# A decoder layer's self-attention: values of two head pairs in one product of 256 columns

## The chip, the core and the metric

The kernel runs on one core of a Trainium2 chip. The metric is device time in microseconds (us) of one execution, smaller is better. A core has five engines that run side by side, each through its own list of instructions in order: TensorE (PE; its weight loads are shown apart as PEld), VectorE (DVE), ScalarE (ACT), GpSimd (POOL) and SyncE (SP), which only starts transfers. They meet by semaphores. Transfers between the core's memories and HBM share 16 DMA engines. PE's results land in PSUM, which PE writes and VectorE and ScalarE read.

## What is computed

One decoder layer in float32: self-attention, cross-attention and a feed-forward block, each followed by a layernorm of input plus result. x has 2 batches of 1024 tokens and 256 channels; there are 16 heads of 64. Only the self-attention is touched:

```python
q = split_heads(x @ Wq)      # Wq, Wk, Wv: 256 x 1024
k = split_heads(x @ Wk)
v = split_heads(x @ Wv)
q = apply_rope(q); k = apply_rope(k)
sim = einsum('bid,bjd->bij', q, k) * scale
attn = softmax(where(causal, sim, -inf), axis=-1)
out = einsum('bij,bjd->bid', attn, v) ... @ Wo + bo
```

## The kernel before

Self-attention goes by *pairs* of heads: 16 pairs, 8 for each batch (`keys`). A pair's columns of Wq, Wk and Wv are 128 wide. The work of a pair is cut into named steps, and the order of all steps on all engines is written out by hand: `steps` is one *period*, a list of (step, further), and period n runs each step for pair n + further. A period holds the scores of pair n, the attention products of pair n - 1 and the projections of pairs n + 1 and n + 2. A text `opening` gives the order before the first full period, and `ending` the order of the last two pairs; steps done there are skipped in the periods. The steps that matter here, with the pair's number in front when one is meant (2e0 is step e0 of pair 2):

- `L`: loads the pair's weights (SP, one DMA for each of Wk, Wq, Wv). `Pk`, `Pq` with a half 0 or 1: projections of 512 tokens on PE (L270). `Ek`, `Eq`: ScalarE copies them out of PSUM to `raw` (L278). `d`, `c`, `s`, `a`: the rope, by a DMA that swaps rows into `turned` and by GpSimd (L296 to L305).
- `Pv0`, `Pv4`: values of tokens 0 to 511 and 512 to 1023 (`values`, L313): 4 tiles of 128 tokens, two products each, with 128 columns of Wv moving. `Ev0`, `Ev4`: ScalarE copies them to the tile `v` (L322), one buffer. `w` (`spread`): stores `v` to HBM (`v_d`, 512 KB). `l` (`copies`, L332): four DMAs of 512 KB bring it back in another layout, `v4`, two issued by ScalarE's queue and two by SP.
- `S0` to `S4`: scores (L353), both heads side by side on two halves of PE's rows. `T`: VectorE masks them and takes the row's extreme (L367), out of two pairs of PSUM banks. `X`: ScalarE's exponentials (L375). `R`: VectorE transposes into `pT` (L384).
- `V0` to `V7`: attention products (L424), 244 small ones a pair from `v4` and `pT` into four PSUM banks, 64 in V0 and V1, 64 in V2 and V3, 116 in V4 to V7; scores of the next pair stand between these three bursts (each product of the program leaves two matmul and two weight-load records). `O`, `M`, `W`: the result is copied, scaled and stored to `attn_d`. `A` loads it for the closing of batch 0, whose `po_proj` products (L496) run in periods 10 and later.

PSUM has a ring of four banks (tag "t") that projections, values, attention products and po_proj take in turn; a product waits until the bank four turns back was copied out. `begin` (L210) starts a DMA on SP; `gate` holds some of them until the attention products V1 or V7 of a pair (or some scores) are through.

`split` cuts a product's columns into 2, or for projections 4, and takes each cut from the pair's budget `pieces`, refilled at V7:

```python
n = 4 if most == 4 and left[0] >= 8 else 2
if left[0] < n - 1 or last - first < n * P:
    return [slice(first, last)]
left[0] -= n - 1
```

`turn_x` turns x into `x_ts` on PE (L193), four blocks of 512 tokens in three buffers.

Of the kernel before, what the change touches and what calls it, by code (L numbers as in the profile page):

```python
# [8 lines left out]
F32 = mybir.dt.float32  # L9
# [7 lines left out]
P, R32 = 128, 32  # L17
B, T, C = 2, 1024, 256
H, D = 16, 64
# [3 lines left out]
NT = T // P  # L23
NC = C // P
NP = INNER // P
NF = FF // P
NB = 512
# [7 lines left out]
def decoder_layer(  # L35
# [24 lines left out]
    V, A, G, TE = nc.vector, nc.scalar, nc.gpsimd, nc.tensor  # L60
# [5 lines left out]
    dram = ctx.enter_context(tc.tile_pool(name="dram", bufs=2, space=DRAM))  # L66
# [58 lines left out]
    keys = [(b, hp) for b in range(B) for hp in range(NP)]  # L125
# [3 lines left out]
    e1 = early.enter_context(tc.tile_pool(name="early1", bufs=1, side="right"))  # L129
    e2 = early.enter_context(tc.tile_pool(name="early2", bufs=2, side="right"))  # L130
    with (
# [76 lines left out]
        def begin(dst, src):  # L208

            ins = nc.sync.dma_start(dst, src)  # L210
            if gate:
                tc.add_manual_dep(ins.ins, gate.pop().ins.name, after, reason="the outputs' instructions come first")
# [3 lines left out]

        pieces = [2, 1, 15, 13, 11, 10, 11, 12, 13, 12, 8, 9, 8, 8, 9, 0]
        left = [pieces[0]]  # L220

        def split(first, last, most):

            n = 4 if most == 4 and left[0] >= 8 else 2
            if left[0] < n - 1 or last - first < n * P:
                return [slice(first, last)]
            left[0] -= n - 1
            step = -(-(last - first) // n // P) * P
            return [slice(m, min(m + step, last)) for m in range(first, last, step)]
# [18 lines left out]
        class Pair:  # L248
            def __init__(self, n):
                self.n, (self.b, self.hp) = n, keys[n]  # L250
                self.pp, self.raw, self.turned, self.p, self.spans, self.marks = {}, {}, {}, {}, {}, {}
                self.w = self.kq = self.v = self.out = None


            def weights(self):
                if self.w is not None:
                    return
                self.w = e2.tile([P, NC, 3, P], F32, tag="w", name="w_pair")
                cols = slice(self.hp * P, (self.hp + 1) * P)
                for i, w in enumerate((L0_attn_Wk, L0_attn_Wq, L0_attn_Wv)):  # L260
                    begin(self.w[:, :, i, :], w.rearrange("(c p) n -> p c n", p=P)[:, :, cols])


# [41 lines left out]
                    E.tensor_tensor(dst, dst, tiles_of(self.turned[n][:, i, :], odd), ALU.add)  # L305


            def values(self, n):
                pv = self.pp["v", n] = ring.tile([P, NT // 2, P], F32, tag="t", name="pp_v")
                for i in range(NT // 2):  # L310
                    toks = slice(i * P, (i + 1) * P)
                    for c in range(NC):
                        TE.matmul(  # L313
                            pv[:, i, :], x_ts[self.b, 2 * n // NT][:, c, toks], self.w[:, c, 2, :],
                            start=(c == 0), stop=(c == NC - 1),
                        )

            def kept(self, n):
                if self.v is None:
                    self.v = e1.tile([P, NT, P], F32, tag="v", name="v")  # L320
                    self.v_d = dram.tile([4, R32, NT * P], F32, tag="v", name="v_d")
                A.copy(self.v[:, n : n + NT // 2, :], self.pp["v", n])  # L322

            def spread(self):

                begin(self.v_d.rearrange("r k e -> (r k) e"), self.v.rearrange("p n d -> p (n d)"))

            def copies(self):

                self.v4 = s1.tile([P, K4, P], F32, tag="v4", name="v4")  # L330
                for r in range(4):
                    (nc.scalar, nc.sync)[r % 2].dma_start(  # L332
                        self.v4[r * R32 : (r + 1) * R32, :, :].rearrange("k (c n) d -> k c (n d)", c=4),
                        self.v_d.rearrange("c k e -> k c e"),
                    )


# [116 lines left out]
            def store(self):  # L454
                begin(
                    attn_d[self.b][self.hp], self.out.rearrange("p t q -> p (t q)")
                )

        class Closing:


# [46 lines left out]


        steps = [  # L510
            ("Eq0", 1), ("Ek0", 1), ("Ev4", 1), ("Eq1", 1), ("a0", 0), ("R40", -1), ("S0", 0), ("T00", 0), ("T01", 0),
            ("s1", 0), ("V0", -1), ("a1", 0), ("V1", -1), ("S1", 0), ("GS1", 0), ("d0", 1), ("V2", -1), ("T10", 0),
            ("V3", -1), ("T11", 0), ("S2", 0), ("GS2", 0), ("B", -2), ("X00", 0), ("V4", -1), ("V5", -1), ("R00", 0),
            ("X01", 0), ("R01", 0), ("c0", 1), ("Z", -15), ("X11", 0), ("T20", 0), ("V6", -1), ("T21", 0), ("V7", -1),
            ("w", 1), ("X10", 0), ("X20", 0), ("O1", -1), ("S3", 0), ("R10", 0), ("O0", -1), ("R11", 0), ("Q", -1),
            ("s0", 1), ("O3", -1), ("T31", 0), ("l", 0), ("C", 0), ("O2", -1), ("X31", 0), ("Pk1", 1), ("T30", 0),
            ("I", -1), ("Pv0", 2), ("X30", 0), ("M", -2), ("R20", 0), ("Ek1", 1), ("d1", 1), ("R31", 0), ("Ev0", 2),
            ("D", -1), ("S4", 0), ("R30", 0), ("Pq1", 2), ("L", 3), ("W", -2), ("A", 0), ("c1", 1), ("X21", 0),
            ("Pq0", 2), ("T41", 0), ("Pk0", 2), ("X41", 0), ("T40", 0), ("R21", 0), ("R41", 0), ("X40", 0), ("Pv4", 2),
        ]  # L520

        pairs = [Pair(n) for n in range(len(keys))]
        acts = {
            "P": lambda a, x: a.values(int(x[1])) if x[0] == "v" else a.project(x[0], int(x[1])),
            "E": lambda a, x: a.kept(int(x[1])) if x[0] == "v" else a.evacuated(x[0], int(x[1])),
            "d": lambda a, x: a.swap(int(x)),
            "c": lambda a, x: a.cosine(int(x)),
            "s": lambda a, x: a.sine(int(x)),
            "a": lambda a, x: a.rotated(int(x)),
            "w": lambda a, x: a.spread(),  # L530
            "l": lambda a, x: a.copies(),
            "L": lambda a, x: a.weights(),
            "S": lambda a, x: a.scores(int(x)),
# [13 lines left out]


        opening = """
            1L 0Pk0 0Ek0 0Pq0 0Eq0 0H 0h 0Pq1 0c0 0d0 0s0 0a0 0Pk1 0Pv4 0Pv0 0Eq1 0S0 0Ek1 0Ev0 1Pk1 0T00 0d1 0Ev4 0T01  # L550
            1Pq1 0X00 0c1 0s1 0X01 1Eq1 1Ek1 1Pv0 0a1 0S1 2L 0R00 0w 0R01 1d1 1Pv4 1c1 1Pq0 1Pk0 0T10 0T11 0S2 1Ev4 0T21
            1Eq0 1Ek0 1d0 0X10 1Ev0 0l 1s1 1w 0X11 2Pq1 0T20 0R10 0S3 0R11 0X21 0X20 0T30 2Pk0 1a1 0T31 0X30 1c0 0S4
            0X31 0R20 1s0 0R30 0R21 1a0 2Eq1 0T40 3L 2Pv4 0T41 2Pv0 0X40 0X41 2Ek0 0R31 0R40 2Pq0 2Ev4 1S0 0R41 1T00
            2Eq0 2Ev0 0V0 1T01 0V1 2d0 0V2 1S1 1T11 0V3 1X00 0V4 0V5 1T10 1S2 1X01 1X11 1R00 0V6 0V7 2w 1X10 0O0 1T20
            1T21 1S3 1R10 1R01 0O1 2c0 1l 1X20 1T31 2Pk1 0O3 1T30 0O2 3Pv4 0Q 2Ek1 1S4 2c1 1X30 2s0 1X21 3Pq1 1R20 3Ev4
            3Pv0 2a0 1R11 3Pk0 0I 1T41 2d1 1R30 1X31 3Pq0 1T40 2S0 1R21 1X41 1X40 1R31 1R40 0D 1R41 2T00 3Ek0 2s1 3Eq1
            4L 2a1 3Eq0 3Ev0 1V0 1V1 3d0 0B 2T01 2X00 1V2 2S1 1V3 1V4 2T10 2T11 1V5 2R00 2S2 2X01 2T20 2T21 1V6 2X11
            2R01 1V7 3c0
        """


        ending = """
            14X10 14X20 14S3 13O0 15s0 15a0 12M 14X21 14R11 14R20 14l 13O1 14T31 14T30 14R21 14X30 14X31 15Pk1 15w 13Q 13I
            14S4 15Ek1 14T40 12W 4C 14T41 14X41 13O2 14R10 15a0 15d1 14R31 13O3 14R30 13D 14X40 15c1 14R40 14R41 15S0 4Y
            15T00 14V0 15T01 15X00 14V1 14V2 15X01 15s1 15a1 14V3 5A 13B 15R00 15S1 15T10 14V4 6A 15X10 14V5 15T11 15S2
            14V6 14V7 15X11 15R01 15T21 15l 15T20 13M 14O3 15S3 7A 15X20 5C 15X21 15R10 15T30 14O0 15T31 15R11 15X30
# [12 lines left out]
        def do(n, step):  # L579
            if (n, step) in done or not 0 <= n < (NT if step in closing else len(keys)):  # L580
                return
            if step in closing:
                b, act = closing[step]
                act(closings[b][n])
            elif step == "H":
                turn_x(0, NH, NT)
            elif step == "h":
                for keep in kept_later:
                    keep()
            elif step == "N":  # L590
                load_cross(n)
            elif step == "n":
                turn_context()
            else:
                if n == last and step[0] == "O":
                    pairs[n].gathered_scaled(int(step[1]))
                elif n == 0 and step in ("c0", "s0", "a0"):
                    {"c": pairs[0].cosine, "s": pairs[0].sine, "a": pairs[0].rotated}[step[0]](0, V)
                else:
                    acts[step[0]](pairs[n], step[1:])  # L600

                if (n, step) in ((NP - 3, "S4"), (NP, "Pv0")):
                    turn_x(1, *((0, NH) if step == "S4" else (NH, NT)))
                if step == "V7" and n + 1 < len(keys):
                    left[0] = pieces[n + 1]
                if step == "W":
                    for f in later.get(n, ()):
                        f()
            done.add((n, step))
# [683 lines left out]
```

## Time and profile before

| what | us |
|---|---|
| median of 3 runs (788.04 to 791.29) | 790.05 |
| the profiled execution | 789.92 |
| its span | 788.2 |
| first attention product (V0 of pair 0) | 51.0 |
| V0 of pairs 1, 2, 3 | 81.1, 111.4, 141.5 |
| V0 of pairs 11, 12, 13, 14, 15 | 384.6, 417.1, 450.1, 475.6, 507.5 |
| PE, records of scores, attention products, kq projections, values (chain share) | 18%, 17%, 14%, 7% |
| a store of `v` (512 KB), issue to landing, median | 8.4 |
| a load to `v4` (512 KB), issue to landing, median | 11.8 (ScalarE's queue), 11.0 (SP's) |

A page of the profile gives each engine's busy time and share; the chain of waits follows the end back from instruction to whatever released it, so that its shares are of time that nothing else hid. A timeline lists the instructions in order (start, length, engine, line, output<-inputs, shapes, count), with the idle time before one in brackets and who ended it; "issue" is a wait for nothing that the profile shows. Ends of matmuls are modelled, so PE's pace is read from starts. The granted clock of PE was 0.996 over the span.

### The profile page before, as it was taken

The page shows a single profiled execution, that of the slowest core. Times are in us where ns is not written, and L with a number is a line of the kernel's source. Part 1 is how long each engine was busy: PE and PEld are TensorE (multiplying, and loading weights), DVE is VectorE, ACT ScalarE, POOL GpSimd, SP SyncE. Part 2 cuts the span into 40 slices and gives each one's busy share as a digit, 9 for nine tenths or more (in the row PEclk, how much of TensorE's full clock was granted, in tenths as well). Part 3 has the DMA queues.
Part 4 walks back from the last instruction along what each step waited for, and adds up shares of the span by engine and source line. Part 5 has one row for each costly group of instructions (what it writes and reads, how often), then busy time and mean ns, then how long its engine had stood idle before and what let it go on. Part 6 is the DMA issues. An engine that isn't in the chain of part 4 may idle for free.

```text
span 788.2 us, 27062 instructions
## 1 busy us (share of the span) xinstructions
PE 762.3 (97%) x11328; PEld 615.8 (78%) x11328; DVE 552.5 (70%) x1299; ACT 390.0 (49%) x1249; POOL 391.0 (50%) x407
## 2 busy tenths in 40 slices
PE   8999999999999999999999998999999999999996
PEld 6565788888888888888887877688967888787755
DVE  2578679669669669677786687815576678758673
ACT  2555566566566566554555553400565665552130
POOL 3733665665575575573754854034024333371665
PEclk9999999999999999999999999999999999999999
DMA  5356377477377577576483656775069988861131
GB/s 200 121 163 173 123 206 196 156 197 201 133 190 198 173 227 190 174 202 178 141 241 112 180 153 175 178 249 178 1 197 238 213 214 204 194 159 54 54 107 53
DMA packets 141413, 131.97 MB, mean 167 GB/s; under 512 B 79554, under 2 KB 117996, under 8 KB 141292
## 3 DMA queue, kind: packets, MB, share of 16 engines
q1 hardware_dynamic: 133132, 100.09, 46.2%
q10 hardware_dynamic: 6624, 25.96, 11.0%
q0 software_dynamic: 1536, 4.20, 1.5%
q8 instruction: 89, 1.46, 0.8%
q14 instruction: 32, 0.26, 0.1%
HBM read 81.68 MB, written 31.76 MB: 144 GB/s over the span
## 4 chain that ended last, share of the span: by engine, by line
PE 81%; POOL 5%; DVE 5%; DMA 4%; issue 3%; ACT 1%; ACTq 0%; POOLq 0%; SPq 0%; DVEq 0%
PE ps_scores L353 18%; PE po_self L424 17%; PE pp_kq L270 14%; PE pp_v L313 7%; PE po_proj L496 6%; PE po_cross L1079 5%; PE ps_cross L1009 5%; PE pp_h L942 2%; POOL comp L877 2%; PE po_ffn L957 2%; POOL e_all L1037 2%; DMA turned<-raw 1%; DVE reach L847 1%; DMA over<-inv_d 1%; PE ps_vo L768 1%
## 5 line engine op out<-in xcount | busy, mean ns | idle before, releaser
L375 ACT ACTIVATE p<-p,neg 128x768 f32<-128x768 f32 (+7 forms) x256 | 196.3, 768 | 148.7 <-DVE neg L367 147.0
L367 DVE CUSTOM_DVE_ANT_0 p<-ps_scores,fence 128x512 f32<-128x512 f32 (+7 forms) x256 | 179.5, 751 | 104.6 <-PE ps_scores L353 104.3
L384 DVE STREAM_TRANSPOSE pT<-p 128x512 f32<-128x512 f32 (+7 forms) x256 | 175.8, 740 | 6.0 <-PE po_self L424 4.1
L424 PE MATMUL po_self<-pT,v 32*64 32x128 f32 (+7 forms) x7808 | 151.1, 290 | 10.2 <-issue 7.7
L424 PEld LDWEIGHTS po_self<-pT,v 32*64 32x64 f32 x7808 | 135.2, 131 | 31.6 <-issue 23.1
L353 PE MATMUL ps_scores<-kq 64*128 64x256 f32 (+3 forms) x1060 | 150.8, 410 | 0.3 <-POOL kq L305 0.3
L353 PEld LDWEIGHTS ps_scores<-kq 64*128 64x128 f32 x1060 | 99.5, 186 | 35.5 <-issue 18.4
L270 PE MATMUL pp_kq<-xT,w_pair 128*128 128x256 f32 (+2 forms) x532 | 118.9, 376 | 1.0 <-ACT xT L194 0.8
L296 POOL TENSOR_TENSOR kq<-raw,cos 128x256 f32<-128x256 f32 (+1 forms) x93 | 82.2, 912 | 60.2 <-ACT raw L278 60.2
L301 POOL TENSOR_TENSOR turned<-turned,sin 128x1024 f32<-128x1024 f32 x31 | 73.2, 2363 | 78.3 <-DMA turned<-raw 78.2
L270 PEld LDWEIGHTS pp_kq<-xT,w_pair 128*128 128x128 f32 x532 | 88.8, 191 | 23.7 <-issue 10.7
L1028 ACT ACTIVATE e_all<-ps_cross,top 128x77 f32<-128x77 f32 x256 | 79.0, 339 | 53.0 <-DVE top L1020 51.0
L1037 POOL TENSOR_TENSOR e_all<-e_all,inv 128x616 f32<-128x616 f32 x32 | 38.8, 1216 | 91.0 <-DVE inv L1035 91.0
L305 POOL TENSOR_TENSOR kq<-kq,turned 128x256 f32<-128x256 f32 (+1 forms) x93 | 82.4, 914 | 1.5
L107 POOL TENSOR_TENSOR rs<-ve,neg_half 128x1 f32<-128x1 f32 x48 | 26.8, 560 | 109.8 <-DVE ve L105 109.5
L1079 PE MATMUL po_cross<-packed,pT 128*128 128x256 f32 (+1 forms) x320 | 72.1, 380 | 0.3 <-issue 0.3
L1009 PE MATMUL ps_cross<-wqk,x1T 128*128 128x308 f32 x256 | 69.9, 425 | 0.3 <-ACT e_all L1028 0.3
L1079 PEld LDWEIGHTS po_cross<-packed,pT 128*128 128x128 f32 (+1 forms) x320 | 60.0, 190 | 9.3 <-issue 0.7
L313 PEld LDWEIGHTS pp_v<-w_pair,xT 128*128 128x128 f32 x512 | 61.1, 192 | 4.0 <-issue 2.5
L313 PE MATMUL pp_v<-w_pair,xT 128*128 128x128 f32 x512 | 62.2, 276 | 0.0
L1009 PEld LDWEIGHTS ps_cross<-wqk,x1T 128*128 128x128 f32 x256 | 47.2, 190 | 17.5 <-ACT e_all L1028 1.3
L1028 ACT ACTIVATION_READ_ACCUMULATOR e_all<-ps_cross,top 128x1 f32 x256 | 56.4, 220 | 0.0
(129 smaller groups left out, 789.2 us busy)
## 6 DMA issues: line engine op xcount, KB each, us to landing
turned<-raw SPq DMA_DIRECT2D x64, 256.0 KB, 5.1
v<-v_d ACTq DMA_DIRECT2D x32, 512.0 KB, 11.8
v<-v_d SPq DMA_DIRECT2D x32, 512.0 KB, 11.0
part_d<-part ACTq DMA_DIRECT2D x14, 640.0 KB, 4.0
pT<-part_d SPq DMA_DIRECT2D x56, 160.0 KB, 3.9
v_d<-v SPq DMA_DIRECT2D x16, 512.0 KB, 8.4
over<-inv_d SPq DMA_DIRECT2D x32, 256.0 KB, 4.4
attn_d<-out_pair SPq DMA_DIRECT2D x14, 512.0 KB, 4.1
```

The costliest lines, as they stand in the source:

```text
L270: TE.matmul(pp[:, cols], self.w[:, c, "kq".index(of), :], x_ts[self.b, n][:, c, cols], start=(c == 0), stop=(c == NC - 1),)
L296: E.tensor_tensor(dst, tiles_of(self.raw[n][:, i, :], odd), tiles_of(cos[:, n * NB : (n + 1) * NB], odd), ALU.mult)
L305: E.tensor_tensor(dst, dst, tiles_of(self.turned[n][:, i, :], odd), ALU.add)
L313: TE.matmul(pv[:, i, :], x_ts[self.b, 2 * n // NT][:, c, toks], self.w[:, c, 2, :], start=(c == 0), stop=(c == NC - 1),)
L353: ins = TE.matmul(self.ps[j][:, cols], self.kq[rows, 1, t * P : (t + 1) * P], self.kq[rows, 0, cols.start - at : cols.stop - at], start=Tr ...
L367: V.tensor_tensor_reduce(p[:, span], self.ps[j][:, span], fences[t % 2][:, T - (t + 1) * P :], -SCALE, -MASKED, ALU.add, ALU.min, neg[:, i ...
L375: A.activation(p[:, span], p[:, span], AF.Exp, bias=neg[:, i : i + 1], scale=-1.0, accum_out=self.sums[:, j, t : t + 1],)
L384: V.transpose(p_t[:, first : first + t * step + 1 : step, :], self.p[g, j][:, span].rearrange("p (n k) -> p n k", k=P),)
L424: ins = TE.matmul(self.po[r][j * D : (j + 1) * D, t:, :], self.v4[rows, NT * k + a, j * D : (j + 1) * D], p_t[rows, first : first + (NT - ...
L1009: TE.matmul(ps[:, g, : Q * S], self.x_t[:, c, :], wqk[:, c, self.b, h : h + Q, :].rearrange("p h s -> p (h s)"), start=(c == 0), stop=(c = ...
L1028: A.activation(self.e[:, hh * HH + h, :], sc[:, g, q, :], AF.Exp, bias=top[:, g, q : q + 1], accum_out=sums[:, h : h + 1],)
L1079: TE.matmul(po, self.p_t[:w, k, :], of[:w, k, :], start=(k == 0), stop=(k == NK - 1))
```

## The change

Two neighbouring pairs make a `Couple`. Its Wv columns, 256 wide, are loaded at once (`i`, one buffer) and are the moving side of one product, so that a product gives 128 tokens' values of both pairs. A period makes half of the tokens for a couple: for an even pair tokens 0 to 511, for an odd one 512 to 1023, in two steps of two token tiles each (`p0`, `p2`), copied out by `e0`, `e2` into `v`, which holds both pairs' half, and stored by `w` into a `v_d` for both pairs. A couple's first pair needs both halves, so the value steps run one pair further ahead (3 instead of 2 for the products, 2 instead of 1 for the store). The halves for pair 9 are done together at `p2` and `e2`, since the block of x that they read is turned later in that period. The budgets of cuts are larger, a four-way cut needs 3 left and not 8, the blocks of batch 1 are turned at S4 of pairs 4 and 6, and the opening is written anew for the couples.

```diff
--- before.py
+++ after.py
@@ pieces and their cuts
-        pieces = [2, 1, 15, 13, 11, 10, 11, 12, 13, 12, 8, 9, 8, 8, 9, 0]
+        pieces = [2, 13, 18, 17, 14, 16, 15, 16, 17, 17, 12, 13, 12, 16, 7, 2]
...
-            n = 4 if most == 4 and left[0] >= 8 else 2
+            n = 4 if most == 4 and left[0] >= 3 else 2
@@ class Pair
-                self.w = e2.tile([P, NC, 3, P], F32, tag="w", name="w_pair")
+                self.w = e2.tile([P, NC, 2, P], F32, tag="w", name="w_pair")
...
-                for i, w in enumerate((L0_attn_Wk, L0_attn_Wq, L0_attn_Wv)):
+                for i, w in enumerate((L0_attn_Wk, L0_attn_Wq)):
...
-            def values(self, n):
-                pv = self.pp["v", n] = ring.tile([P, NT // 2, P], F32, tag="t", name="pp_v")
-                for i in range(NT // 2):
-                    toks = slice(i * P, (i + 1) * P)
-                    for c in range(NC):
-                        TE.matmul(
-                            pv[:, i, :], x_ts[self.b, 2 * n // NT][:, c, toks], self.w[:, c, 2, :],
-                            start=(c == 0), stop=(c == NC - 1),
-                        )
-
-            def kept(self, n):
-                if self.v is None:
-                    self.v = e1.tile([P, NT, P], F32, tag="v", name="v")
-                    self.v_d = dram.tile([4, R32, NT * P], F32, tag="v", name="v_d")
-                A.copy(self.v[:, n : n + NT // 2, :], self.pp["v", n])
-
-            def spread(self):
-
-                begin(self.v_d.rearrange("r k e -> (r k) e"), self.v.rearrange("p n d -> p (n d)"))
-
             def copies(self):
...
-                        self.v_d.rearrange("c k e -> k c e"),
+                        couples[self.n // 2].v_d[self.n % 2].rearrange("c k e -> k c e"),
@@ new
+        class Couple:
+            def __init__(self, m):
+                self.b, self.hp = keys[2 * m]
+                self.pp, self.w, self.v_d, self.v = {}, None, None, {}
+
+            def weights(self):
+                if self.w is not None:
+                    return
+                self.w = e1.tile([P, NC, 2 * P], F32, tag="wv", name="w_values")
+                cols = slice(self.hp * P, (self.hp + 2) * P)
+                begin(self.w, L0_attn_Wv.rearrange("(c p) n -> p c n", p=P)[:, :, cols])
+
+            def values(self, n):
+                pv = self.pp[n] = ring.tile([P, 2, 2 * P], F32, tag="t", name="pp_v")
+                for i in range(2):
+                    at = (n + i) * P % NB
+                    for c in range(NC):
+                        TE.matmul(
+                            pv[:, i, :], x_ts[self.b, n // NH][:, c, at : at + P], self.w[:, c, :],
+                            start=(c == 0), stop=(c == NC - 1),
+                        )
+
+            def kept(self, n):
+                h, i = divmod(n, NH)
+                if h not in self.v:
+                    self.v[h] = e1.tile([P, 2, NH, P], F32, tag="v", name="v")
+                A.copy(
+                    self.v[h][:, :, i : i + 2, :].rearrange("p j i d -> p i j d"),
+                    self.pp[n].rearrange("p i (j d) -> p i j d", j=2),
+                )
+
+            def spread(self, h):
+                if self.v_d is None:
+                    self.v_d = dram.tile([2, 4, R32, NT * P], F32, tag="v", name="v_d")
+                begin(
+                    self.v_d.rearrange("j r k e -> (r k) j e")[:, :, h * NB : (h + 1) * NB],
+                    self.v[h].rearrange("p j i d -> p j (i d)"),
+                )
@@ steps of a period (the lines with a changed step)
-            ("Eq0", 1), ("Ek0", 1), ("Ev4", 1), ("Eq1", 1), ("a0", 0), ("R40", -1), ("S0", 0), ("T00", 0), ("T01", 0),
+            ("Eq0", 1), ("Ek0", 1), ("e2", 2), ("Eq1", 1), ("a0", 0), ("R40", -1), ("S0", 0), ("T00", 0), ("T01", 0),
...
-            ("w", 1), ("X10", 0), ("X20", 0), ("O1", -1), ("S3", 0), ("R10", 0), ("O0", -1), ("R11", 0), ("Q", -1),
+            ("w", 2), ("X10", 0), ("X20", 0), ("O1", -1), ("S3", 0), ("R10", 0), ("O0", -1), ("R11", 0), ("Q", -1),
...
-            ("I", -1), ("Pv0", 2), ("X30", 0), ("M", -2), ("R20", 0), ("Ek1", 1), ("d1", 1), ("R31", 0), ("Ev0", 2),
-            ("D", -1), ("S4", 0), ("R30", 0), ("Pq1", 2), ("L", 3), ("W", -2), ("A", 0), ("c1", 1), ("X21", 0),
-            ("Pq0", 2), ("T41", 0), ("Pk0", 2), ("X41", 0), ("T40", 0), ("R21", 0), ("R41", 0), ("X40", 0), ("Pv4", 2),
+            ("I", -1), ("p0", 3), ("X30", 0), ("M", -2), ("R20", 0), ("Ek1", 1), ("d1", 1), ("R31", 0), ("e0", 3),
+            ("D", -1), ("S4", 0), ("R30", 0), ("Pq1", 2), ("i", 4), ("L", 3), ("W", -2), ("A", 0), ("c1", 1), ("X21", 0),
+            ("Pq0", 2), ("T41", 0), ("Pk0", 2), ("X41", 0), ("T40", 0), ("R21", 0), ("R41", 0), ("X40", 0), ("p2", 3),
...
+        couples = [Couple(m) for m in range(len(keys) // 2)]
+        of_couples = {
+            "p0": lambda a, h: a.values(h * NH), "p2": lambda a, h: a.values(h * NH + 2), "e0": lambda a, h: a.kept(h * NH),
+            "e2": lambda a, h: a.kept(h * NH + 2), "w": lambda a, h: a.spread(h), "i": lambda a, h: h or a.weights(),
+        }
@@ opening (its first lines) and ending
-            1L 0Pk0 0Ek0 0Pq0 0Eq0 0H 0h 0Pq1 0c0 0d0 0s0 0a0 0Pk1 0Pv4 0Pv0 0Eq1 0S0 0Ek1 0Ev0 1Pk1 0T00 0d1 0Ev4 0T01
-            1Pq1 0X00 0c1 0s1 0X01 1Eq1 1Ek1 1Pv0 0a1 0S1 2L 0R00 0w 0R01 1d1 1Pv4 1c1 1Pq0 1Pk0 0T10 0T11 0S2 1Ev4 0T21
-            1Eq0 1Ek0 1d0 0X10 1Ev0 0l 1s1 1w 0X11 2Pq1 0T20 0R10 0S3 0R11 0X21 0X20 0T30 2Pk0 1a1 0T31 0X30 1c0 0S4
-            0X31 0R20 1s0 0R30 0R21 1a0 2Eq1 0T40 3L 2Pv4 0T41 2Pv0 0X40 0X41 2Ek0 0R31 0R40 2Pq0 2Ev4 1S0 0R41 1T00
+            1L 0i 0Pk0 0Ek0 0Pq0 0Eq0 0H 0h 0Pq1 0c0 0d0 0s0 0a0 0Pk1 0p0 0p2 0Eq1 0S0 0Ek1 0e0 0e2 1Pk1 0T00 0d1 1p0 0w 1p2 0T01
+            1Pq1 0X00 0c1 0s1 0X01 1Eq1 1Ek1 0a1 0S1 2i 2L 0R00 1e0 1e2 1w 0R01 1d1 2p0 2p2 1c1 1Pq0 1Pk0 0T10 0T11 0S2 2e0 2e2 0T21
+            1Eq0 1Ek0 1d0 0X10 0l 1s1 2w 0X11 2Pq1 0T20 0R10 0S3 0R11 0X21 0X20 0T30 2Pk0 1a1 0T31 0X30 1c0 0S4
+            0X31 0R20 1s0 0R30 0R21 1a0 2Eq1 0T40 3L 3p0 3p2 0T41 0X40 0X41 2Ek0 0R31 0R40 2Pq0 3e0 3e2 4i 1S0 0R41 1T00
...
-            14X10 14X20 14S3 13O0 15s0 15a0 12M 14X21 14R11 14R20 14l 13O1 14T31 14T30 14R21 14X30 14X31 15Pk1 15w 13Q 13I
+            14X10 14X20 14S3 13O0 15s0 15a0 12M 14X21 14R11 14R20 14l 13O1 14T31 14T30 14R21 14X30 14X31 15Pk1 13Q 13I
@@ do()
+            elif (n, step) in ((NP + 1, "p0"), (NP + 1, "e0")):
+                return
+            elif step in of_couples:
+                for one in (step[0] + "0", step) if (n, step) in ((NP + 1, "p2"), (NP + 1, "e2")) else (step,):
+                    of_couples[one](couples[n // 2], n % 2)
...
-                if (n, step) in ((NP - 3, "S4"), (NP, "Pv0")):
-                    turn_x(1, *((0, NH) if step == "S4" else (NH, NT)))
+                if (n, step) in ((NP - 4, "S4"), (NP - 2, "S4")):
+                    turn_x(1, *((0, NH) if n == NP - 4 else (NH, NT)))
```

## The prediction

> **What bounds the kernel now.** I read the page's busy shares first, then the chain of waits in order of time, then the timelines of single engines, then the stretches from one first attention product to the next. PE is busy in 97% of the span and makes up 81% of the chain. Between 1.5 and 465 us the chain is PE nearly without a break, so in self-attention time is PE's own pace, plus what holds PE up.
>
> ```profile
> PE 762.3 (97%) x11328; PEld 615.8 (78%) x11328; DVE 552.5 (70%) x1299; ACT 390.0 (49%) x1249; POOL 391.0 (50%) x407
> PE 81%; POOL 5%; DVE 5%; DMA 4%; issue 3%; ACT 1%; ACTq 0%; POOLq 0%; SPq 0%; DVEq 0%
> ...
> q8 instruction: 89, 1.46, 0.8%
> ```
>
> ```profile
> 37.43 1.80 PE ps_scores L353 x8
> 39.23 1.91 PE pp_kq L270 x4
> 41.14 2.71 PE ps_scores L353 x8
> ...
> 275.29 1.79 PE pp_kq L270 x16
> 277.08 1.79 PE pp_v L313 x16
> 278.87 1.93 PE ps_scores L353 x16
> 280.80 5.38 PE pp_kq L270 x24
> 286.18 1.78 PE pp_v L313 x16
> ...
> 334.12 3.46 PE po_proj L496 x16
> ```
>
> The chain gives paces (start, us, work, records; an f32 product leaves two records). Sixteen value records of 128 columns take 1.79 us, 111.9 ns each. Sixteen records of 256 columns (po_proj) take 3.46, 216.25 each. A projection of 512 columns cut in four (16 records) takes 1.79, and cut in two 8 x 216.25 = 1.73.
>
> What holds PE up within a period is seen in its timeline, at pairs 2 and 7. It is the burst V4 to V7, once split by a hole and once whole:
>
> ```profile
> 123.88 1.34 PE L424 MATMUL po_self<-pT,v 32*64 32x64 f32 x104 [1.02 <-issue]
> ```
>
> ```profile
> 270.06 3.31 PE L424 MATMUL po_self<-pT,v 32*64 32x128 f32 x232
> ```
>
> The hole waits for no other engine. The instruction queue moved 1.46 MB in 89 packets, 16.4 KB each, which at 22,656 PE instructions is 255 instructions a packet: PE waits for its own code. From the start of such a burst to the scores behind it takes 4.28 us at pair 2 (120.87 to 125.15) and 3.24 at pair 7 (270.06 to 273.30). Over pairs 2 to 13 these holes come to about 4 us.
>
> The last view is VectorE at the end of pair 12's period, and the two last full periods as windows (length, then busy us of PE, PEld, DVE, ACT, POOL):
>
> ```profile
> 444.11 3.21 DVE L384 STREAM_TRANSPOSE pT<-p 128x768 f32<-128x768 f32 x3
> 450.18 0.69 DVE L367 CUSTOM_DVE_ANT_0 p<-ps_scores,fence 128x512 f32<-128x512 f32 x1 [2.85 <-PE ps_scores L353]
> ```
>
> ```profile
> 417.10:450.10 33.00, 32.45 (x639) 27.30 (x637) 24.07 (x54) 17.27 (x42) 18.90 (x19) 1.00 0.52 162
> 450.10:475.60 25.50, 24.09 (x588) 19.70 (x586) 22.00 (x50) 14.37 (x37) 14.13 (x14) 1.00 0.56 152
> ```
>
> VectorE ends its transposes at 447.3 and PE starts the next attention products at 450.1. So here PE has the last word by 2.8 us. The period after it has no values left, and there VectorE is busy for 22.0 of 25.5.
>
> **The change, part by part**, against the profiled execution: span 788.2, time 789.92, so 1.7 outside the span. The median of the three runs, 790.05, is 0.1 above it.
>
> *Values.* 512 records of 128 columns become 256 of 256: 512 x 111.9 = 57.3 against 256 x 216.25 = 55.4, all on the chain: -1.9 us.
>
> The Trainium skill (TensorE: Matmul & The Clock Gate, Back-to-back issue gap) puts a warm matmul at its columns over 2.4 GHz plus 2.5 ns, which would make each merge worth 2.5 ns and all 256 of them 0.6 us (an estimate). The rows give 2 x 111.9 - 216.25 = 7.5 ns a merge.
>
> *Cuts.* `pieces` goes from 142 to 207 in sum, and four-way cuts are allowed from 3 left, not 8. Counted in the two programs' order, projections cut in four rise from 9 to 45, those in two fall from 42 to 8; 36 x (1.79 - 1.73) = +2.2. Scores lose 18 products, some 5 ns each: -0.1. Together +2.1, on the chain. What the cuts buy is place: 128 products fewer in values against 65 x 2 more from cuts leave PE's program as long as it was (5742 against 5740 products), and from pair 1 on each pair's attention products start within 0.06 of a 256-instruction block of where they did. So I let the holes stay. Were all lost, -4.1.
>
> The Trainium skill (Runtime: NRT & Kernel Launch, Instruction fetch mechanics) calls a 16 KiB boundary mostly hidden; by that the holes would be nothing and the cuts a plain loss of 2.1. The 1.02 us above is against it.
>
> *One half-couple moves from the end to the opening.* A period now makes half the tokens for two pairs, so both halves must be there before the couple's first pair. Before the first attention product (51.05) stand 96 value records now, 96 x 111.9 = 10.7, and then 64 of the wide ones, 13.8: +3.1 there, and 32 narrow ones (-3.6) fewer in pair 12's period. As sums these are in the first term; what matters is what stands beside them.
> - Opening: PE waits there for VectorE to free score banks: 2.71 us for 8 score records that take 1.92 elsewhere, and 1.80 for 8 that need some 1.6. More PE work ahead covers this: -1.0. Against it, there is one `v` buffer, and ScalarE's copy 2e0 now waits for the store 1w, with 1Eq0, 1Ek0 and pair 0's exponentials behind it; then 3e0 for 2w, which shares the engines with 2 MB of v4 loads. Before, the store issued at 37.56 released ScalarE at 49.15 (11.6 us) and cost 0.20. I put 2w near 40, so its landing near 51.7, three copies of 0.59 behind it to 53.5; PE arrives at 51.05 + 3.1 - 1.0 = 53.1. Those 0.4 I leave out; bounds -1.0 to +2.0, value -1.0.
> - End: pair 12's period loses 3.6 of PE work and gains 0.2 of cuts, while VectorE's end left only 2.8: 0.6 is not earned. Bounds 0 and 3.4 (all of it, if scores come no earlier): +0.6.
>
> *Pair 0's code.* Its products start a quarter block earlier (1.73 against 1.98). Two holes stand in them now, at 60.69 (0.64) and 64.52 (0.56). With that shift one boundary leaves the second burst. Bounds -1.2 and +1.0, value -0.4.
>
> *Loads and stores.* Wv comes as 256 KB for two pairs instead of 128 KB for each, v_d leaves in runs of 2 KB instead of 4: equal bytes, off the chain. But the step `i` (five times from pair 6 on) waits on SP for a buffer that the same period's last value product still reads. So Wv, the next pair's Wk and Wq, the attention store and an x or attnT load, issued at 104 to 109 in pair 2's period, all go at about 109.7: 256 + 256 + 512 + 512 KB, at 167 to 200 GB/s done by 117.5 to 119, and the 512 KB of `turned`, gated at 115.5, after them by 120.5 to 122. None is needed early: weights a period later, `turned` 10 us later. They are covered until 120.9, where V4 to V7, the code-hungry burst, begins. With that cover gone the price is a longer hole, up to 1.04 (4.28 - 3.24) five times: 0 to +5; I take 0.2 each, +1.0.
>
> *ScalarE, VectorE, GpSimd.* As many copies as before, of the same 512 elements (586 ns), with 512-byte runs in another order: 0; if a copy took 20% more, ScalarE's 17 of 30 us a period hide it.
>
> Sum: -1.9 + 2.1 - 1.0 + 0.6 - 0.4 + 1.0 = +0.4, so 789.92 + 0.4 = **790.3 us**.
>
> **Rivals.**
> 1. *Slower: the blocked SP queue.* The late loads run into V4 to V7 at each of the five `i`, and the code comes late. It decides once the backlog ends after 121, that is at under some 180 GB/s for its 2 MB. For it: the page's mean of 167. Against it: V0 and V1 took 3.27 us with or without 0.5 MB beside them. With 1.04 each and the opening's +2.0 instead of -1.0: 790.3 + 4.2 + 3.0 = 797.5; half of it is 794.
> 2. *Faster: holes close.* If the new alignment ends them, -4.1, and pair 0 gains 1.2: 790.3 - 4.1 - 0.8 = 785.4. For it: pairs 7 and 9 show whole bursts. Against it: starts move by less than 0.06 block.
> 3. *The end pays nothing* (VectorE bound in pair 12's period): +2.8, 793.1, still within 0.5%. Against it: 24.07 busy of 33.
>
> **How the numbers follow.** What a measurement of this kernel tells from no change is 0.5%, 3.95 us. The forecast, with rival 3 in it, has 0.68, its own range 787 to 793.5. The slower case has 0.18 and the faster 0.14. Leaving 0.1 out on either side gives 786 to 795.
>
> **What would show it.** Right: value records at 216 ns and a pair's V-to-V distance within 0.3 us of before in pairs 2 to 11; first attention product near 53; pair 12's period near 30 us; the holes behind 120.9 of like size. Wrong: ScalarE idle over 3 us before a copy to `v` from 50 on (opening); holes over 1 us in every second period (SP); V-to-V shorter by 0.3 throughout (holes gone). A wait of a value product for `w_values` would break the whole account.

## The result, and the profile after

The changed kernel takes 794.52 us (median of 8 runs, 792.52 to 797.76) against 790.22 (8 runs, 788.04 to 792.39) in the same job: ratio 1.0059, 95% interval [1.0042, 1.0077], some 4.3 us slower. 790.3 was forecast, with a range of 786 to 795. The profiled execution, 792.52 with a span of 790.7, is the shortest of its eight; its mean granted clock is 0.998, that of the other seven 0.991 to 0.994. In the experiments below, executions more than 1.5% above the fastest of their kernel are left out of the ratios (the medians have all); two profiles (`again`, `end_place`) are of such long executions, and are read only for where time goes.

The page after, the lines that answer to those of the prediction (busy time, chain, the instruction queue):

```profile
PE 762.7 (96%) x11332; PEld 612.0 (77%) x11332; DVE 552.6 (70%) x1299; ACT 390.4 (49%) x1249; POOL 390.5 (49%) x407
...
q8 instruction: 89, 1.46, 0.8%
...
PE 81%; DVE 7%; POOL 5%; issue 4%; ACT 1%; DMA 1%; POOLq 0%; SPq 0%; ACTq 0%; DVEq 0%
```

PE is busy 0.4 us longer (762.7 against 762.3), though the span grew by 2.6. The two terms of PE's own work, values -1.9 and cuts +2.1, come out as summed: from one start to the next, the same amount of values takes mostly 1.82 us (8 records of 256 columns) where it took 1.88 (16 of 128), and the longest group of projections in a middle period 5.30 to 5.46 where it took 5.28. So what the change cost is mostly waiting. First attention products (V0) cut the spans into stretches, in us:

| stretch | before | after | difference |
|---|---|---|---|
| start to V0 of pair 0 | 50.98 | 54.07 | +3.09 |
| to V0 of pair 2 | 60.46 | 59.00 | -1.46 |
| to V0 of pair 12 | 305.70 | 308.18 | +2.48 |
| to V0 of pair 13 | 32.95 | 30.00 | -2.95 |
| to V0 of pair 15 | 57.38 | 55.32 | -2.06 |
| to the end of the span | 280.69 | 284.18 | +3.48 |

The fifth row is not the change's: in the profile before, the granted clock was 0.88 from 470 to 480 us and 0.95 from 480 to 490, 1.7 us lost; in the one after it was 1.00 there, but `wv_late` and `best_a` below, which have the change, show the dip again (0.91 and 0.89 from 470 to 480). Without the dip the sum would be +4.3, as between the medians; that the two agree may be luck, since the other seven executions after had a lower clock than the profiled one.

*Opening.* PE's timeline after (start, length, instructions):

```profile
40.57 1.87 PE L333 MATMUL ps_scores<-kq 64*128 64x512 f32 x8
...
44.29 2.77 PE L333 MATMUL ps_scores<-kq 64*128 64x512 f32 x8
...
54.07 4.25 PE L404 MATMUL po_self<-pT,v 32*64 32x256 f32 x174
```

From their starts to the next, S3 and S4 take 1.80 and 2.70 us, so their two waits are as long as before. Why, VectorE's timelines show, after and then before, at the first mask of the group that S2 made:

```profile
38.78 0.96 DVE L347 CUSTOM_DVE_ANT_0 p<-ps_scores,fence 128x768 f32<-128x768 f32 x1 [6.06 <-PE ps_scores L333]
```

```profile
35.56 0.96 DVE L367 CUSTOM_DVE_ANT_0 p<-ps_scores,fence 128x768 f32<-128x768 f32 x1 [4.39 <-PE ps_scores L353]
```

VectorE itself waited for S2, and started 3.2 us later. The added value products stand ahead of S2, so they push PE and VectorE alike, and the two meet at S3 and S4 as before.

*Pair 2.* The burst V4 to V7 in PE's timeline after, and the stretches V0 to V1, from there to V4, and V4 to V7 as windows (length, busy us of PE, PEld, DVE, ACT, POOL, then granted clock, share of the DMA engines and GB/s):

```profile
122.49 1.99 PE L404 MATMUL po_self<-pT,v 32*64 32x128 f32 x132
126.97 1.31 PE L404 MATMUL po_self<-pT,v 32*64 32x64 f32 x100 [2.49 <-issue]
```

```profile
113.07:116.34 3.27, 3.27 (x132) 2.88 (x130) 2.42 (x12) 2.44 (x9) 3.19 (x5) 1.00 0.96 283
116.34:122.49 6.15, 6.15 (x156) 4.48 (x148) 4.13 (x12) 2.81 (x9) 2.64 (x4) 1.00 0.49 177
122.49:128.21 5.72, 3.23 (x233) 3.05 (x233) 4.83 (x11) 1.98 (x6) 3.19 (x2) 1.00 0.36 95
```

From one start to the next 2.7 us pass (2.49 of them idle, against 1.02 in this burst before) in which PE waits for nothing the profile shows: a hole in its code. The DMA engines are full in V0 and V1 (0.96), where PE doesn't suffer; it suffers 10 us later.

*Behind the last V0.* PE's timeline after, where it lost time to before:

```profile
516.31 1.56 PE L519 MATMUL po_proj<-wo,attnT 128*128 128x256 f32 x6 [0.70 <-issue]
...
551.38 4.44 PE L747 MATMUL pp_k<-cxT,w_k 128*128 128x154 f32 x32 [0.63 <-issue]
...
708.46 4.56 PE L1111 MATMUL po_cross<-packed,pT 128*128 128x256 f32 x20 [1.48 <-issue]
```

None of these was in the prediction.

### The profile page after: what moved, and what is told of

It is laid out like the page before. It is cut to its first block, busy times and chain, and to the rows that moved or that the text cites. A ratio compares the mean times of both kernels' runs of the same rounds, so it can differ in the third digit from the quotient of the medians.

```text
span 790.7 us, 27049 instructions
## 1 busy us (share of the span) xinstructions
PE 762.7 (96%) x11332; PEld 612.0 (77%) x11332; DVE 552.6 (70%) x1299; ACT 390.4 (49%) x1249; POOL 390.5 (49%) x407
## 3 DMA queue, kind: packets, MB, share of 16 engines
q8 instruction: 89, 1.46, 0.8%
## 4 chain that ended last, share of the span: by engine, by line
PE 81%; DVE 7%; POOL 5%; issue 4%; ACT 1%; DMA 1%; POOLq 0%; SPq 0%; ACTq 0%; DVEq 0%
PE ps_scores L333 18%; PE po_self L404 17%; PE pp_kq L270 14%; PE pp_v L459 7%; PE po_proj L519 6%; PE po_cross L1111 5%; PE ps_cross L1041 4%; PE pp_h L974 2%; POOL e_all L1069 2%; PE po_ffn L989 2%; DVE reach L879 2%; POOL comp L909 2%; DVE part L1076 1%; DVE pT L364 1%; PE ps_vo L800 1%
## 5 line engine op out<-in xcount | busy, mean ns | idle before, releaser
L404 PE MATMUL po_self<-pT,v 32*64 32x128 f32 (+7 forms) x7808 | 149.0, 288 | 11.5 <-issue 8.8
L270 PE MATMUL pp_kq<-xT,w_pair 128*128 128x128 f32 (+2 forms) x828 | 120.9, 302 | 1.1 <-ACT xT L194 1.0
L270 PEld LDWEIGHTS pp_kq<-xT,w_pair 128*128 128x128 f32 x828 | 102.1, 192 | 14.7 <-issue 9.7
L459 PE MATMUL pp_v<-w_values,xT 128*128 128x256 f32 x256 | 59.9, 380 | 0.0
L459 PEld LDWEIGHTS pp_v<-w_values,xT 128*128 128x128 f32 x256 | 47.1, 190 | 8.2 <-issue 1.2
```

The source lines that it names most:

```text
L270: TE.matmul(pp[:, cols], self.w[:, c, "kq".index(of), :], x_ts[self.b, n][:, c, cols], start=(c == 0), stop=(c == NC - 1),)
L404: ins = TE.matmul(self.po[r][j * D : (j + 1) * D, t:, :], self.v4[rows, NT * k + a, j * D : (j + 1) * D], p_t[rows, first : first + (NT - ...
L459: TE.matmul(pv[:, i, :], x_ts[self.b, n // NH][:, c, at : at + P], self.w[:, c, :], start=(c == 0), stop=(c == NC - 1),)
```

## The experiments

Theories. A: the load of Wv blocks SP, the loads behind it fill the DMA engines, and the fetches of PE's code come late. B: PE's instructions have moved within their 256-instruction blocks. C: it is the added work (cuts, opening).

### Wv's load out of the way, and the changed kernel again

```diff
-            ("D", -1), ("S4", 0), ("R30", 0), ("Pq1", 2), ("i", 4), ("L", 3), ...
+            ("D", -1), ("S4", 0), ("R30", 0), ("Pq1", 2), ("L", 3), ...
-            ..., ("X40", 0), ("p2", 3),
+            ..., ("X40", 0), ("p2", 3), ("i", 4),
```

> The changed kernel once more, for a second profile. The profiled execution after lost, against the one before, 3.1 us up to the first attention product, 2.7 in a hole of PE's code at pair 2 (126.97), and some 3.4 between the last pair's first attention product and the end (holes of 0.70, 1.13, 0.63, 0.3 and 1.48 us put down to issue), and it had no stretch of lowered clock where before had 0.94 and 0.97 from 460 to 500 us. If the holes belong to the program, they stand at the same places here, each within 0.3 us, and the stretch behind the last pair's first attention product is again near 284.1 (before 280.7). If they are chance, they move, and that stretch comes out anywhere from 281 to 284. Time near 794.5 either way; a run with the clock at 0.994 should be some 2 us longer than the one profiled.

> Only the load of Wv moves on SP, from in front of the next pair's Wk and Wq to behind the period's last value product, so that it blocks nothing. Theory of the blocked SP queue: the 2.7 us hole at pair 2 and the 1.3 us hole at pair 8 go, the bytes that leave in V0 and V1 of every second period fall from 1.0-1.1 MB to the 0.5 MB of before, and the time falls by 3 to 4 us, to about 791. Theory of the place of the code alone: holes and time stay, 794.5 within 1 us.

Again: 801.02 (6 runs), 1.0108 [1.0063, 1.0152], longer than expected. Of the holes behind the last V0, those in po_proj (0.70, here 1.07) and ahead of pp_k (0.63) came again, the 1.48 in the cross-attention did not. With the load moved: 794.92 (12 runs), 1.0036 [1.0011, 1.0061], some 6 us under `again` on the same chip. SP's timelines around pair 2, the changed kernel and then the one with the load moved:

```profile
104.64 0.80 SPq L210 DMA_DIRECT2D inv_d<-inv  x1
111.44 0.40 SPq L210 DMA_DIRECT2D w_values<-in_L_attn_Wv_dram  x1
111.87 0.47 SPq L210 DMA_DIRECT2D w_pair<-in_L_attn_Wk_dram  x1
...
113.37 0.34 SPq L210 DMA_DIRECT2D attn_d<-out_pair  x1
```

```profile
105.95 0.54 SPq L210 DMA_DIRECT2D inv_d<-inv  x1
106.61 0.40 SPq L210 DMA_DIRECT2D w_pair<-in_L_attn_Wk_dram  x1
...
109.37 0.34 SPq L210 DMA_DIRECT2D attn_d<-out_pair  x1
...
112.31 0.37 SPq L210 DMA_DIRECT2D w_values<-in_L_attn_Wv_dram  x1
```

SP stood still for 6 us and then sent everything into V0 and V1. Moved, the same windows read 118 GB/s where it was 283, and the burst is whole:

```profile
113.94:117.21 3.27, 3.27 (x131) 2.88 (x129) 2.42 (x12) 2.43 (x9) 3.19 (x5) 1.00 0.36 118
...
123.37:126.55 3.18, 3.18 (x234) 3.05 (x233) 3.18 (x9) 1.97 (x6) 1.02 (x1) 1.00 0.57 170
```

V0 to V0 in us, the five periods with the load of Wv and, for control, the five others from pair 1 on:

| kernel | pairs 2, 4, 6, 8, 10 | sum | pairs 1, 3, 5, 7, 9, sum |
|---|---|---|---|
| before | 30.03 30.45 29.32 29.82 32.79 | 152.4 | 151.1 |
| after | 31.51 29.26 29.33 30.17 32.86 | 153.1 | 152.4 |
| again | 33.07 29.81 34.57 32.67 35.38 | 165.5 | 152.7 |
| wv_late | 28.97 29.54 29.55 29.62 32.64 | 150.3 | 152.9 |

In the control the three kernels of the change agree within 0.5; the blocked periods cost 2.8 us in the profile after and 15.2 in the long execution. From V0 of pair 2 to V0 of pair 12 the kernel with the load moved takes 305.57, before 305.70. Theory A holds for the middle of the kernel; 1.0036 is left for the rest.

The packets of the instruction queue show the way from the load to the hole. In most periods the first three fetches behind V0 start near 1.0, 4.6 and 9.1 us after it. In pair 2 of the changed kernel they start at 1.4, 6.5 and 11.5, in pair 6 of `again` at 1.8, 6.6 and 11.7. So a late fetch can delay the next, and the third is the one that V4 to V7 run out on. It need not: in pair 6 of the changed kernel the first started at 2.2, the third at 9.4, and only a hole of 0.3 us followed.

### The same block in the kernel before

> The kernel before with one move only: the SP steps that load the next pair's weights, store attn_d and load x or attnT stand behind Pv4, the last step of a period, instead of behind Pq1. No PE instruction changes. Theory of late loads (in the runs so far the five periods in which the changed kernel blocks SP took 2.8, 15.2 and 13.4 us more, in sum, than with Wv's load out of the way, 0.6 to 3 us a period): every period from pair 1 to pair 12 now has its loads beside V0 to V3, the fetches of PE's code come late, holes of 1 to 3 us open in V4 to V7, some with a stretch of half clock behind them, and the time rises by 6 to 33 us. Theory that the couples' program itself makes the holes: no change, within 2 us of before.

793.73 (12 runs), 1.0003 [0.998, 1.0026]. This edit did nothing: SP waits only for what a transfer needs, no other SP step lies between the two places, and Wk left at 104.54 where it had left at 103.98. So the wait had to be added too:

```diff
-            ..., ("Pq1", 2), ("L", 3), ("W", -2), ("A", 0), ("c1", 1), ...
+            ..., ("Pq1", 2), ("c1", 1), ...
-            ..., ("Pv4", 2),
+            ..., ("Pv4", 2), ("GP4", 2), ("L", 3), ("W", -2), ("A", 0),
...
-                        TE.matmul(
+                        self.marks["P", n] = TE.matmul(
```

> The kernel before, its weight loads, attn_d store and x or attnT load behind Pv4 on SP, and the first of them made to wait for Pv4's last product, as the changed kernel's load of Wv does (moved without that wait, SP issued them at the same times as before and nothing changed, 1.0003 of before). PE's instructions are those of before. Theory of the blocked SP queue: in every period from pair 2 to pair 12 these loads leave at the end of the period, 0.5 MB more beside V0 and V1; the holes in V4 to V7, 0 to 1.2 us now, become 2 to 3 us in part of the periods, some with half clock behind, 0.6 to 3 us a period: 797 to 825. Theory that the blocking hurts only with the couples' program: within 2 us of before.

804.95 (6 runs), 1.0178 [1.0137, 1.0219]: 14 us for a wait on a queue that computes nothing, with PE's instructions unchanged. SP at pair 10, and the windows there:

```profile
350.18 0.54 SPq L210 DMA_DIRECT2D inv_d<-inv  x1
357.41 0.40 SPq L210 DMA_DIRECT2D w_pair<-in_L_attn_Wk_dram  x1
...
359.39 0.43 SPq L210 DMA_DIRECT2D attnT<-attn_d  x1
```

```profile
359.02:362.29 3.27, 3.27 (x130) 2.87 (x129) 2.42 (x12) 2.43 (x9) 3.17 (x4) 1.00 0.96 298
...
371.00:372.00 1.00, 0.00 (x0) 0.00 (x0) 1.00 (x5) 0.85 (x2) 0.00 (x0) 1.00 0.33 78
372.00:373.00 1.00, 0.00 (x0) 0.00 (x0) 1.00 (x2) 0.18 (x2) 0.00 (x0) 0.94 0.04 12
373.00:374.00 1.00, 0.88 (x59) 0.88 (x64) 1.00 (x3) 0.00 (x0) 0.00 (x0) 0.50 0.00 0
...
378.00:379.00 1.00, 1.00 (x8) 0.68 (x6) 0.52 (x1) 0.00 (x0) 0.00 (x0) 0.50 0.82 336
```

PE is idle from 370.6 to 373.1, and then runs at a granted clock of 0.50 for over 6 us, though busy. So a missed fetch can cost twice: the hole, and some 3 us behind it. Holes of 2.7 to 3.1 us stand at pairs 4, 7, 10 and 13, where the first fetch behind V0 started at 2.5 to 3.2 us and the third at 11.6 to 11.9; in the other periods from pair 1 to 12 the third started at 9.1 to 9.8, and they differ little from before. Theory A is shown without the couples.

### What the cuts are for

```diff
-        pieces = [2, 13, 18, 17, 14, 16, 15, 16, 17, 17, 12, 13, 12, 16, 7, 2]
+        pieces = [2, 1, 15, 13, 11, 10, 11, 12, 13, 12, 8, 9, 8, 8, 9, 0]
-            n = 4 if most == 4 and left[0] >= 3 else 2
+            n = 4 if most == 4 and left[0] >= 8 else 2
```

> The changed kernel with the cuts of before (142 in sum, four-way only from 8 left); PE's program is 129 products (2 blocks) shorter and each pair's attention products start at another place of their block. If the added cuts are a plain cost: 36 projections x 0.06 = 2.1 us less, 792.4. If they buy the place of the attention products: the holes in V4 to V7 grow at the pairs whose place moves most (pairs 2 to 5 and 8 to 13), by 0 to 1 us each, and the time goes to 795 to 799.

830.6 (6 runs), 1.0489 [1.0446, 1.0532], far above both expectations. With Wv's load moved as well:

> Wv's load out of the way and the cuts of before. The changed kernel with the cuts of before took 830.6, 36 more. If that came of the code's place in the blocks (pairs 2, 3, 4 and 8 to 12, whose attention products start at 0.08 to 0.18 and 0.29 to 0.60 of a block, took 32 to 38 us each), most of it stays: 815 to 828, and the same pairs are long. If it came of the blocked SP queue meeting a program without slack, it goes: 793 to 797.

827.51 (6 runs), 1.0435 [1.0395, 1.0475]. Taking 2.1 us of cuts out of PE's work costs some 30 us, wherever the load stands (1.0489 against 1.0108, 1.0435 against 1.0036). In the second run pairs 2, 3, 4 and 7 to 12 have holes of 2.5 to 3.4 us in V4 to V7. So the cuts are more than a cost to be weighed against the values' gain: with the old ones this order of steps loses some 30 us. This run changes the number of instructions along with their place, so the place was moved alone:

```diff
-            fill(2)
+            fill(1, 17)
...
+            for _ in range(narrow):
+                TE.matmul(t[:, :1], ident, ident[:, :1], start=True, stop=True)
```

> Wv's load out of the way; of the two wide products that PE runs on nothing at the start one is replaced by 17 of one column, so that every later PE instruction stands 64 instructions (a quarter block) further on; cuts as changed. Theory of the code's place: pairs 6 to 12, whose attention products now start at 0.10 to 0.19 of a block, lose 2 to 4.5 us each, as pairs 2 to 4 did with the cuts of before, and the time is 809 to 825. If place is worth nothing and the old cuts cost for another reason, the time stays near 795, at most 2 more for a later start.

845.2 (6 runs), 1.0648 [1.0608, 1.0688], far outside what was expected. 6.6 us of it is the edit itself (34 records of one column took 7.1 us at the start, V0 came at 60.71). The rest is place: V0 of pair 2 to V0 of pair 12 takes 337.7 against 305.6, and pairs 1 to 13 all have holes of 2.4 to 3.0 us. Pair 6 in PE's timeline:

```profile
267.55 3.10 PE L406 MATMUL po_self<-pT,v 32*64 32x128 f32 x226
273.16 0.31 PE L406 MATMUL po_self<-pT,v 32*64 32x32 f32 x6 [2.50 <-issue]
```

By the place of the hole, the block's edge now lies six records before the burst's end, with nothing but attention products ahead of it.

### The end and the opening

> One product of a single column is added to the fill ahead of the last pair's attention products; with it every PE instruction behind it stands at the same place in its 256-instruction block as before the change (the changed kernel had them 4 instructions earlier). Theory of the code's place: the holes behind 507 us go (0.70, 1.13, 0.63, 1.48), the stretch from the last pair's first attention product to the end falls from 284.1 to about 281, and the time by 3 us, to 791.5. Theory of late loads, or of chance: no change there, 794.5 within 1 us.

798.0 (10 runs), 1.0067 [1.0032, 1.0101]; its last V4 to V7 still had a hole of 1.5 us, and the stretch behind the last V0 did not shrink. So putting these instructions back to the place that they had before does not cure the end, and theory B in that form is wrong there. Two other edits, on the kernel with Wv's load moved:

```diff
-            ... 1c0 0S4
+            ... 1c0 3p0 0S4
-            ... 0T40 3L 3p0 3p2 0T41 ...
+            ... 0T40 3L 3p2 0T41 ...
-            ... 15Q 2= 14D
+            ... 15Q 1= 1= 14D
```

> Wv's load out of the way, 3p0 moved ahead of 0S4 (there PE waits some 0.9 us for VectorE), and the fill at the end split into two tiles of the ring, so that the cross attention's first product falls on another bank than the last po_proj (it waited 0.8 us for VectorE to read that bank in every run of the changed kernel, 28.5 against 27.7 us from the first of the last po_proj to it). Expected: first attention product near 53.3 instead of 54.1, the wait ahead of pp_k gone, time 1.6 less than with Wv's load moved alone, 793.3; if the waits only move on, no less.

794.11 (12 runs), 1.0008 [0.9984, 1.0033]: level with before, though not clear of the 1.0036 with the load moved alone. PE's timeline, S4 and the hand-over to the cross-attention:

```profile
44.20 1.89 PE L459 MATMUL pp_v<-w_values,xT 128*128 128x256 f32 x8
46.02 1.99 PE L333 MATMUL ps_scores<-kq 64*128 64x512 f32 x8
...
551.48 1.03 PE L519 MATMUL po_proj<-wo,out_pair 128*128 128x256 f32 x4
552.34 4.36 PE L747 MATMUL pp_k<-cxT,w_k 128*128 128x154 f32 x32
```

S4 takes 1.92 from start to start, not 2.70; V0 comes at 53.38, 0.7 earlier. The wait ahead of pp_k is gone: from the first of the last four po_proj records to it 0.86 us pass, as before the change, against 1.66 in the changed kernel and in each variant of it without the two fills. In the changed kernel pp_k starts at 551.38, just after VectorE has read the last po_proj result (550.86 to 551.28); here it starts at 552.34, ahead of that read (552.61). The order of the ring's tiles had turned by one bank.

### How wide the place is

The version above, and the kernel before, with all PE instructions 16 later (`fill(1, 5)`), and the version with them 16 earlier (`pieces[0]` 0, not 2):

> The version that came to 1.0008 of before, with all its PE instructions behind the start moved 16 on (a sixteenth of a block), by five products of one column in place of one wide one on nothing. A quarter block on, each V4 to V7 had a hole of 2.4 to 3.0 us; a seventh of a block back, pair 7 had one of 3.4; an eighth on, pair 5 had none where it has 0.5. If the place in use has its holes of 0.4 to 0.8 because a fetch comes just too late, and more slack lies ahead, they shrink and the time falls by 2 to 4 us, to 788 to 791 beside a before of 791 to 793; if the place is near its edge on that side, periods of the later pairs jump by 2 to 4 us each and the time is 800 to 830.

> The same 16 instructions in the kernel before: its attention products stand within 0.06 of a block of the changed kernel's, so the answer should have the same sign and size as the other's.

> The version that came to 1.0008 of before, with pieces[0] 0 in place of 2: the first pair's two two-way cuts are left out, so that all PE instructions behind them stand 16 earlier (a sixteenth of a block). Sixteen later cost 11 to 14 us in both kernels. If the place in use stands close to that edge, 16 earlier gives the fetches more slack, the holes of 0.4 to 0.8 in V4 to V7 shrink, and the time is 1 to 3 us under that version's, 788 to 790 where before is 790.8. If the window is narrow on both sides (pair 7, with the old cuts 31 instructions earlier, had a hole of 3.4 us), periods of 32 to 35 us appear and the time is 800 or more.

802.49 (6 runs), 1.0147 [1.0122, 1.0172]; 804.47 (6 runs), 1.0165 [1.0134, 1.0196]; 799.69 (8 runs), 1.0081 [1.0045, 1.0117]. 1.3 us of the first comes from the edit (V0 at 54.63). No version beat the kernel before. Sixteen earlier, pairs 5 and 9 got holes of 2.2 and 2.9 us (V4 to V7 at 211.4 and 334.9), and the stretch behind the last V0 took 285.2 instead of 282.2. Sixteen later, the holes in V4 to V7 did not grow; the time went elsewhere, as pair 9 of the kernel before, so moved, shows in PE's timeline:

```profile
339.57 1.78 PE L355 MATMUL ps_scores<-kq 64*128 64x256 f32 x15
342.45 0.27 PE L355 MATMUL ps_scores<-kq 64*128 64x128 f32 x1 [1.10 <-issue]
```

By the place of this hole, another edge, which had fallen 16 instructions further on, in the slower po_proj products, now falls on the last score behind V7.

## Why the prediction came out as it did

The time lay in the range, near its upper edge, and the sign of the shift was right, which at +0.4 says little; its size, +0.4 against +4.3, was not, and the number that came nearest is half of rival 1 (794).

- *Values -1.9, cuts +2.1:* right. Sixteen value records take 3.45 to 3.65 us in the chain; with the SP queue free, pairs 2 to 11 take 305.57 against 305.70. That the cuts buy place was right; but only the holes in sight were priced (4.1 us), while losing the place costs some 30.
- *Opening waits covered, -1.0:* wrong, 0. The step that failed is "More PE work ahead covers this": the work was put ahead of S2, which VectorE waits for, not between S2 and S4. Moved there in part, it was worth 0.7. ScalarE's wait for the store of `v` was small, as said (0.58 us at 52.42).
- *End, +0.6 not earned:* right (2.95 gained of 3.6 - 0.2). VectorE's last transposes end at 451.09 and PE starts V0 at 451.25, so VectorE now has the last word. Its timeline, and the window of pair 12's period, with VectorE the third engine:

```profile
447.88 3.21 DVE L364 STREAM_TRANSPOSE pT<-p 128x768 f32<-128x768 f32 x3
```

```profile
421.24:451.25 30.01, 29.74 (x636) 25.03 (x634) 24.25 (x54) 16.09 (x40) 16.27 (x16) 1.00 0.61 178
```

- *Pair 0's code, -0.4:* right in sign; its two holes are gone and the period is 0.83 shorter. Pair 1's is 0.63 shorter too, which the sum has no term for; why was not looked into.
- *Late loads through SP, +1.0:* the mechanism was right and the size was wrong. The sum took "a longer hole, up to 1.04" five times, because 1.04 was the longest in the trace before. A fetch that misses V4 to V7 altogether makes a hole of 2.6 to 3.1, and half clock may follow. It was +2.8 in the profiled execution against the kernel with the load moved, with holes over 1 us in two of the five periods, and more in others (801.0 against 794.9 on one chip). The argument that V0 and V1 don't suffer from 0.5 MB beside them was true and beside the point: they have code in hand, and it is the third fetch behind them that is late.
- *Not in the sum:* +3.5 behind the last V0, the largest single error of the profiled execution; the sum has no term for it. 0.8 is the turned bank (shown), 0.9 a hole between V3 and V4 of the last pair, the rest holes in the cross-attention that differ from profile to profile: the 1.48 at 708 is in neither `again`, `wv_late` nor `best_a`.
- *Rival 2* (holes close) did not happen: from pair 2 to pair 13 the holes in V4 to V7 come to 5.8 us, measured as the prediction did, 4.1 before and 4.0 with the load moved. *Rival 3* did not either.

Two places of the Trainium skill bear on this. Runtime: NRT & Kernel Launch, Instruction fetch mechanics, says that the sequencer fetches the next block while it runs the current one and that the edge is mostly hidden; here it is not, since 16 instructions more ahead of everything made the kernel before 13.6 us slower, of which the edit's own work is under 2 (V0 at 52.69 instead of 50.98).

TensorE: Matmul & The Clock Gate, Part 1, says that the gate watches a free-running window of some 3.4 us, and halves the clock after an idle one. The halving and its chance agree: the hole of 2.70 at pair 2 after was followed by clock 1.00, one of 2.63 at the same place in `again` by 0.50. But the holes that did it are shorter than the window named. The traces say more. Where a profile has several stretches of 0.50 ahead of its last microseconds, they start on one grid of 3.41 us and last one or two steps of it. Over the 13 profiles that have any, a step in which PE was idle for more than 0.54 of it was followed by one at 0.50 in 40 of 40 cases, from 0.36 to 0.54 in 12 of 47, below 0.36 in none of 2875 (steps already at 0.50 left out; ends of matmuls are modelled). At pair 2 the hole of `again` fell mostly in one step, idle for 0.70 of it; in the profile after it lay in two, 0.46 and 0.27. So what looks like chance is where the hole falls on the grid.

What stays open: the trace has no time at which a fetch was asked for, so that a fetch waits behind data already queued is read from its late start and not seen directly; and whether cuts planned anew for the version that came level would beat the kernel before wasn't tried.

## What to carry to other kernels

In a kernel bound by PE with dense small products, PE's code is one more stream through the DMA engines: look for the bursts that eat instructions fastest, see where the block edges fall in them, and keep large transfers out of the 10 us ahead. A transfer that waits for a buffer holds everything behind it on its queue, so put it last, and price the queue behind it by what its bytes will then run beside, not by when they are needed. Work moved ahead of a wait covers it only if the engine waited for isn't pushed as well.

## What was not expected of the hardware

- The value of an instruction's place: 16 instructions (4 products) later cost some 10 and 12 us of 790, 64 later some 42, beside the edit's own work.
- A hole of 2.6 to 3.1 us in PE's work is often followed by 3.4 or 6.8 us at a granted clock of 0.50, with PE busy. Shorter ones seldom were, but one of 1.3 at pair 10 of `again` was (0.50 from 380.58): PE idle for more than 0.54 of a 3.41 us step was always enough.
- At the start a record of one column took 209 ns (34 in 7.1 us), where one of 512 took 930 (two in 1.86); later 256 columns take 216. The profile has no record of the clock for this time (it begins at 14.8 us in `wv_late_shift`), so whether the clock was low there is not shown.
